# Output stores on GpSimd's queue and seven load buffers in the transformer stage of a Fourier tokenizer

## The chip, the cores and the metric

The kernel runs on one core of a Trainium2 chip. The metric is the device time of one execution in microseconds (us): the median of several runs. Three runs of the kernel before gave 12764.55, 12770.84 and 12775.92 us, so the time to compare with is 12770.84 us. One further execution was profiled; its trace spans 12772.9 us, and all times inside the trace are counted from its start.

## The reference

The input is 64 images of 256 x 256 and, for each, 77 text rows of 256. Everything is float32. Cut to what matters:

```
v = concat(x, gx, gy) @ p_w + p_b                      # 32 channels
for i in range(4):                                     # Fourier layers
    v = irfft2(low modes of rfft2(v) mixed over channels) + (v @ w_w[i] + w_b[i])
    v = batch_norm(v);  v = relu(v) if i < 3 else v
h = squeeze(v @ q_w + q_b)                             # one channel: 256 rows of 256
h = concat(h, txt)                                     # 333 rows (tokens) of 256
h = h + attention(layer_norm(h))                       # one head, width 256
z = layer_norm(h)
w = z @ wr + br;  the 165 tokens with the largest w are kept
h = h + z + scatter(w * mlp(z[kept]))                  # mlp: 256 -> 1024, gelu, -> 256
```

The batch norm's sums run over all images, so a Fourier layer must be done for all 64 images before the next can begin.

## The kernel before, in words

**The Fourier layers** (`forward_first`, `mix_weights`, `mix`, `layer`) take the first 9.8 ms. The change doesn't touch them. The last layer's image is never made in full: the transformer stage works from what layer 2 left in DRAM (`src`, 8 MB for each image) and from the mixed modes of layer 3 (`mix_d[L - 1]`, 48 x 1024 floats for each image).

**The transformer stage** is one loop over the 64 images. For one image:

- `image_rows` makes the one-channel image. L858 loads the mixed modes `am`. L860 multiplies them by `qrow` into the tile `amq`, and L864 sums over channels to `a1`. TensorE takes two small transforms (L866, L871) into the PSUM tile `hp`. Then for t = 0 to 7, L876 loads a tile `ch` of 1 MB (128 partitions x 8 KB) from `src`, and four matmuls of L878 add it to `hp`. The `ch` tiles come from the pool `inp`, which has five buffers, so five loads can be ahead of TensorE. When all eight tiles are in, ScalarE writes `h` (L883), and L884 loads the text rows into it.
- `attention` normalizes `h` (statistics L892/L893, square root on ScalarE L895, `az` L900), transposes it (L910, copied out of PSUM to `azT`, one half by ScalarE at L168 and the other by VectorE at L170), and goes on with L956 (scores' weights), L968 (scores), L975 (exp), L982 (values), L997 (transposed probabilities) and L1006. L1002 adds the bias `boB` to `h` on GpSimd, and L1009 adds the attention's result.
- `select` ranks the tokens: L922 to L927 put the weights of all tokens into a row on every partition, and nine VectorE instructions for each of three token groups (L936 to L947) count who is larger and write the one-hot tile `place`.
- `feed_forward` gathers the kept tokens (L1024, L1035), runs the two layers of the mlp (L1041, L1052), transposes back (L1062, copied to `ys`), scatters with L1071 and adds in L1074 to the tile `o`. Sixteen stores of 16 KB (L1079) and one of 77 KB (L1083) write `o` to the output.

**What sets the order.** The loop runs three images at once: in one turn it issues `image_rows(b + 2)`, `attention(b + 1)`, `feed_forward(b)` and `select(b + 1)`. The framework's planner merges these into one fixed order for each engine, from its own estimate of when each instruction's inputs are there; then it adds the semaphore waits. Each engine, and each queue of DMA issues, works strictly in that order. All loads and all stores of this stage are issued by SyncE (SP), whose queue is therefore shared: a store that waits for `o` holds back every load behind it. GpSimd has only L1002 and L1067 (`h1 += z`) in this stage, three instructions of each for an image.

Of the kernel before, what the change touches and what calls it, by code (L numbers as in the profile page):

```python
# [9 lines left out]
F32 = mybir.dt.float32  # L10
AF = mybir.ActivationFunctionType
ALU = mybir.AluOpType
# [4 lines left out]
S = 256  # L17
C = 32
M = 12
KX = 2 * M  # L20
L = 4
TXT = 77
TOK = S + TXT
HID = 1024
EPS = 1e-5
KEPT = max(1, int(0.5 * TOK)) - 1
# [103 lines left out]
def tile_fno_fusion_transformer(ctx: ExitStack, tc: tile.TileContext, a, cst_d, grid_d, out):  # L130
    nc = tc.nc
# [626 lines left out]
    src = vd[L % 2]  # L758
    s_, t_ = st
    tcon = ctx.enter_context(tc.tile_pool(name="tcon", bufs=1))  # L760
    inp = ctx.enter_context(tc.tile_pool(name="inp", bufs=5))
    tabt = tables(tcon, "exT", "tri", "cstt")
    EXT, MASK4, IOTA = tabt("exT"), tabt("mask4"), tabt("iota")
    TRI = tabt("tri").rearrange("p (t j) -> p t j", t=3)
    qrow = tcon.tile([128, C, 1], F32, name="qrow")
# [3 lines left out]
    junk = tcon.tile([128, C], F32, name="junkq")  # L769
# [78 lines left out]
    ap_ = ctx.enter_context(tc.tile_pool(name="ta", bufs=2))  # L848
    tp = ctx.enter_context(tc.tile_pool(name="tt", bufs=2))
# [3 lines left out]
    def psum():  # L853
        return pp.tile([128, 512], F32, name="pp")

    def image_rows(b):
        am = ap_.tile([2 * KX, 32 * C], F32, name="am")
        nc.sync.dma_start(am, mix_d[L - 1][b].rearrange("p k c -> (p k) c"))  # L858
        tmp = ap_.tile([2 * KX, C, 32], F32, name="amq")
        nc.vector.tensor_tensor(  # L860
            tmp, am.rearrange("p (o k) -> p o k", k=32), qrow[0:2 * KX].to_broadcast([2 * KX, C, 32]), ALU.mult
        )
        a1 = ap_.tile([2 * KX, 32], F32, name="a1")
        nc.vector.reduce_sum(a1, tmp.rearrange("p o k -> p k o"), axis=AX.X)  # L864
        ps = psum()
        nc.tensor.matmul(ps[0:32, 0:S], lhsT=a1, rhs=EXT[0:2 * KX], start=True, stop=True)  # L866
        y1 = ap_.tile([32, 2, 128], F32, name="y1")
        evict(y1.rearrange("k t p -> k (t p)"), ps[0:32, 0:S], 2)
        hp = pb_.tile([128, 2, S], F32, name="hp")
        for t in range(2):  # L870
            nc.tensor.matmul(  # L871
                hp[:, t, :], lhsT=y1[:, t, :], rhs=T4[0:32], start=t == 0, stop=False, skip_group_check=True
            )
        for t in range(8):
            ch = inp.tile([128, 4, 2, S], F32, name="ch")
            nc.sync.dma_start(ch.rearrange("p g r y -> p (g r) y"), src[b][:, t])  # L876
            for g in range(4):
                nc.tensor.matmul(  # L878
                    hp[32 * g:32 * g + 32], lhsT=win[:, 7 - t:39 - t], rhs=ch[:, g], start=False, stop=t == 7,
                    skip_group_check=True,  # L880
                )
        h = tp.tile([128, 3, D], F32, name="h")
        nc.scalar.activation(h[:, 0:2, :], hp, AF.Identity, bias=hbias, scale=1.0)  # L883
        nc.sync.dma_start(h[0:TXT, 2, :], a["txt"][b])  # L884
        return h
# [28 lines left out]
    def select(z):  # L914


        wcol = small.tile([128, 3], F32, name="wcol")
        ps = psum()
        for t in range(3):
            r = rows[t]  # L920
            junk = tp.tile([128, TOK], F32, name="junk")
            nc.vector.scalar_tensor_tensor(  # L922
                junk[:r, :D], z[:r, t, :], 1.0, wrB[:r], ALU.mult, ALU.mult, accum_out=wcol[:r, t:t + 1]
            )
            dg = tp.tile([128, 128], F32, name="dg")
            nc.vector.tensor_scalar(dg[:r, :r], ID[:r, :r], wcol[:r, t:t + 1], None, ALU.mult)
            nc.tensor.matmul(ps[:, toks[t]], lhsT=ONES[:r], rhs=dg[:r, :r], start=True, stop=True)  # L927
        wrow = tp.tile([128, TOK], F32, name="wrow")
        nc.vector.tensor_scalar(wrow, ps[:, :TOK], brB, None, ALU.add)
        fw = small.tile([128, 3], F32, name="fw")  # L930
        place = tp.tile([128, 3, KEPT], F32, name="place")
        for t in range(3):
            r = rows[t]
            junk = tp.tile([128, TOK], F32, name="junk")
            wc = small.tile([128, 1], F32, name="wc")
            nc.vector.scalar_tensor_tensor(  # L936
                junk[:r, :r], wrow[:r, toks[t]], 1.0, ID[:r, :r], ALU.mult, ALU.mult, accum_out=wc[:r]
            )
            gt = small.tile([128, 1], F32, name="gt")
            nc.vector.tensor_scalar(junk[:r], wrow[:r], wc[:r], None, ALU.is_gt, ALU.add, accum_out=gt[:r])  # L940
            eq = small.tile([128, 1], F32, name="eq")
            nc.vector.scalar_tensor_tensor(
                junk[:r], wrow[:r], wc[:r], TRI[:r, t, :], ALU.is_equal, ALU.mult, accum_out=eq[:r]
            )
            nc.vector.tensor_add(gt[:r], gt[:r], eq[:r])
            nc.vector.tensor_scalar(fw[:r, t:t + 1], gt[:r], float(KEPT), wc[:r], ALU.is_lt, ALU.mult)
            nc.vector.tensor_scalar(place[:r, t, :], IOTA[:r], gt[:r], None, ALU.is_equal)  # L947
        return fw, place
# [68 lines left out]
    def feed_forward(b, h1, z, fw, place):  # L1017

        zs = tp.tile([128, 2, KEPT], F32, name="zs")
        for dh in range(2):  # L1020
            ps = psum()
            for t in range(3):
                r = rows[t]
                nc.tensor.matmul(  # L1024
                    ps[:, :KEPT], lhsT=z[:r, t, 128 * dh:128 * dh + 128], rhs=place[:r, t, :],
                    start=t == 0, stop=t == 2,
                )
            evict(zs[:, dh, :], ps[:, :KEPT], 2)
        back = tp.tile([128, 2, TOK], F32, name="back")
        for c, k in enumerate(kept):  # L1030
            n = k.stop - k.start
            ps = psum()
            for t in range(3):
                r = rows[t]
                nc.tensor.transpose(ps[:n, toks[t]], place[:r, t, k], ID[:r, :r])  # L1035
            evict(back[:n, c, :], ps[:n, :TOK], 2)
        g = tp.tile([128, HID // 128, KEPT], F32, name="g")
        for hb in range(HID // 128):
            ps = psum()
            for dh in range(2):  # L1040
                nc.tensor.matmul(  # L1041
                    ps[:, :KEPT], lhsT=w1[:, dh, 128 * hb:128 * hb + 128], rhs=zs[:, dh, :],
                    start=dh == 0, stop=dh == 1,
                )
            nc.scalar.activation(
                g[:, hb, :], ps[:, :KEPT], AF.Gelu_apprx_tanh, bias=b1c[:, hb:hb + 1], scale=1.0
            )
        yT = tp.tile([128, 2, KEPT], F32, name="yT")
        for dh in range(2):
            ps = psum()  # L1050
            for hb in range(HID // 128):
                nc.tensor.matmul(  # L1052
                    ps[:, :KEPT], lhsT=w2[:, hb, 128 * dh:128 * dh + 128], rhs=g[:, hb, :],
                    start=hb == 0, stop=hb == HID // 128 - 1,
                )
            nc.scalar.activation(yT[:, dh, :], ps[:, :KEPT], AF.Identity, bias=b2c[:, dh:dh + 1], scale=1.0)
        ys = tp.tile([128, 2, D], F32, name="ys")
        for c, k in enumerate(kept):
            n = k.stop - k.start
            ps = psum()  # L1060
            for dh in range(2):
                nc.tensor.transpose(ps[:n, 128 * dh:128 * dh + 128], yT[:, dh, k], ID)  # L1062
            evict(ys[:n, c, :], ps[:n, :D], 2)
        o = tp.tile([128, 3, D], F32, name="o")
        for t in range(3):
            r = rows[t]
            nc.gpsimd.tensor_add(h1[:r, t, :], h1[:r, t, :], z[:r, t, :])  # L1067
            ps = psum()
            for c, k in enumerate(kept):
                n = k.stop - k.start  # L1070
                nc.tensor.matmul(  # L1071
                    ps[:r, :D], lhsT=back[:n, c, toks[t]], rhs=ys[:n, c, :], start=c == 0, stop=c == 1
                )
            nc.vector.scalar_tensor_tensor(  # L1074
                o[:r, t, :], ps[:r, :D], fw[:r, t:t + 1], h1[:r, t, :], ALU.mult, ALU.add
            )
        for g in range(4):
            for n in range(4):
                nc.sync.dma_start(  # L1079
                    out[b, 64 * n + 16 * g:64 * n + 16 * g + 16].rearrange("(p t) d -> p t d", t=2),  # L1080
                    o[32 * g + 8 * n:32 * g + 8 * n + 8, 0:2, :],
                )
        nc.sync.dma_start(out[b, S:TOK], o[0:TXT, 2, :])  # L1083

    hs = {n: image_rows(n) for n in range(min(2, B))}
    done = attention(hs.pop(0))
# [43 lines left out]
```

## Time and profile before

| Stretch or engine | measured |
| --- | --- |
| whole span | 12772.9 us |
| Fourier layers and their weights | to about 9880 us |
| transformer stage, first L1071 to last L1071 | 9969.9 to 12762.0 us |
| TensorE busy, of 2800 us from 9900 on | 2620.5 us |
| VectorE busy, same stretch | 1664.7 us |
| ScalarE busy, same stretch | 962.5 us |
| GpSimd busy, same stretch | 319.8 us |
| DMA engines, mean share in 10000 to 12500 us | 0.53 to 0.56 |

In these views PE is TensorE's matmuls and PEld its weight loads, DVE is VectorE, ACT is ScalarE, POOL is GpSimd, SPq is SyncE's queue. A timeline row gives start, length, engine, source line, operation, tiles written and read, the number of instructions merged into it, and in brackets the idle time of the engine before it with what ended that. A row of the waits gives the waiting engine and line, what it waited for, the total, how often, and the longest. In a table of stretches the columns after the engines' busy times are the clock granted to TensorE, the busy share of the DMA engines and their GB/s. A float32 matmul shows as two instructions, a transpose as one.

### The profile page before, as it was taken

How to read it: one execution, taken by the hardware profiler on the slowest of the kernel's cores; microseconds unless marked ns; L12 is line 12 of the kernel's file. 1: busy time of each engine (PE TensorE's matmuls, PEld its weight loads, DVE VectorE, ACT ScalarE, POOL GpSimd, SP SyncE). 2: the span in 40 equal slices, each digit the busy share in tenths (PEclk: the TensorE clock that was granted, in tenths of full speed). 3: DMA queues.
4: the chain of work that ended last, by engine and by line, in shares of the span. 5: the costliest groups of instructions: out<-in, count | busy, mean ns of one | idle time of the engine just before them, and what ended most of it. 6: DMA issues, size and time to landing. Idle time of an engine off the chain costs nothing. (4 is left out here: it accounts for less than half of the span.)

```text
span 12772.9 us, 405290 instructions
## 1 busy us (share of the span) xinstructions
PE 11352.8 (89%) x182038; PEld 5910.2 (46%) x182038; DVE 8759.3 (69%) x10531; ACT 6084.0 (48%) x10221; POOL 1010.8 (8%) x952
## 2 busy tenths in 40 slices
PE   4999999997799999999969999999995999999999
PEld 2444444443344444444434444444443666666666
DVE  4777777776777767677767777677775655555555
ACT  4555555555455555555545555455553333333333
POOL 1000000001100000000010000000001111111111
PEclk7999999998899999999979999999997999999999
DMA  6555555556899989888888988889988655555554
GB/s 189 201 204 205 198 198 204 199 203 204 326 354 350 352 342 348 341 344 345 345 284 345 356 343 347 341 347 353 351 348 279 218 192 202 206 203 198 191 198 158
DMA packets 574645, 3484.98 MB, mean 273 GB/s; under 512 B 79848, under 2 KB 133352, under 8 KB 175976
## 3 DMA queue, kind: packets, MB, share of 16 engines
q1 hardware_dynamic: 562304, 3427.04, 70.8%
q0 software_dynamic: 2304, 28.30, 1.0%
q8 instruction: 1424, 23.33, 0.7%
q10 hardware_dynamic: 8296, 3.72, 0.1%
q14 instruction: 317, 2.60, 0.1%
HBM read 1761.83 MB, written 1696.92 MB: 271 GB/s over the span
## 5 line engine op out<-in xcount | busy, mean ns | idle before, releaser
L656 ACT ACTIVATE ring<-ring 128x1024 f32<-128x1024 f32 x3072 | 3108.8, 1012 | 1184.6 <-PE ring L649 1147.8
L637 DVE STREAM_TRANSPOSE t<-vo 128x2048 f32<-128x2048 f32 x1536 | 3549.9, 2311 | 173.8 <-ACT vo L632 12.2
L649 PE MATMUL ring<-vo,w 32*32 32x512 f32 x49152 | 2840.7, 622 | 385.6 <-DVE zt L676 136.7
L632 ACT ACTIVATE vo<-ring 128x1024 f32<-128x1024 f32 x1536 | 1568.1, 1021 | 3052.2 <-PE ring L625 2393.8
L633 DVE TENSOR_SCALAR vo<-ring 128x1024 f32<-128x1024 f32 x1536 | 1858.4, 1210 | 615.8 <-PE ring L625 427.2
L666 PE MATMUL ring<-t,cst 32*32 32x512 f32 x49152 | 1872.9, 604 | 305.5 <-issue 303.7
L676 DVE STREAM_TRANSPOSE zt<-ring 128x1024 f32<-128x1024 f32 x384 | 712.1, 1925 | 1657.1 <-PE ring L666 1657.1
L649 PEld LDWEIGHTS ring<-vo,w 32*32 32x32 f32 x49152 | 763.7, 105 | 1892.5 <-issue 477.4
L666 PEld LDWEIGHTS ring<-t,cst 32*32 32x32 f32 x49152 | 974.9, 103 | 1162.8 <-issue 706.8
L625 PE MATMUL ring<-vin,ws 32*32 32x512 f32 x32768 | 1241.9, 608 | 22.2 <-issue 19.7
L584 POOL TENSOR_TENSOR ams<-am,sk 48x512 f32<-48x512 f32 x384 | 486.8, 1268 | 8541.3 <-DMA am<-mix 8199.5
L689 PEld LDWEIGHTS ring<-cst,zt 128*128 128x128 f32 x4608 | 534.7, 193 | 177.2 <-ACT vo L632 161.2
L656 ACT ACTIVATION_READ_ACCUMULATOR ring<-ring 128x1 f32 x3072 | 584.1, 190 | 0.0
L689 PE MATMUL ring<-cst,zt 128*128 128x96 f32 x4608 | 566.9, 280 | 8.8 <-DVE zt L676 8.8
L878 PE MATMUL hp<-ch,win 128*32 128x512 f32 x4096 | 537.2, 619 | 4.9 <-DMA ch<-v 4.9
L595 PE MATMUL ring<-ams,cst 49*128 49x512 f32 (+1 forms) x1536 | 391.6, 620 | 99.2 <-POOL ams L584 88.8
L625 PEld LDWEIGHTS ring<-vin,ws 32*32 32x32 f32 x32768 | 253.5, 103 | 408.3 <-issue 378.8
L892 DVE BATCH_NORM_STATS2 abs<-h 128x6 f32<-128x256 f32 (+1 forms) x192 | 75.8, 402 | 439.1 <-ACT h L883 439.1
L1041 PEld LDWEIGHTS pp<-zs,w 128*128 128x128 f32 x2048 | 291.3, 190 | 99.2 <-issue 68.8
L1041 PE MATMUL pp<-zs,w 128*128 128x165 f32 x2048 | 332.2, 310 | 0.0
L1052 PEld LDWEIGHTS pp<-g,w 128*128 128x128 f32 x2048 | 292.5, 189 | 73.6 <-issue 68.8
L412 PE MATMUL mps<-wm,xh 32*64 32x128 f32 (+1 forms) x4608 | 110.2, 356 | 239.6 <-DMA xh<-xh 109.0
(930 smaller groups left out, 11717.9 us busy)
## 6 DMA issues: line engine op xcount, KB each, us to landing
v<-vo SPq DMA_DIRECT2D x1536, 1024.0 KB
vin<-v SPq DMA_DIRECT2D x1024, 1024.0 KB
ch<-v SPq DMA_DIRECT2D x512, 1024.0 KB
mix<-ob SPq DMA_DIRECT2D x192, 256.0 KB
am<-mix SPq DMA_DIRECT2D x384, 96.0 KB
xin<-in_x_dram SPq DMA_DIRECT2D x16, 1024.0 KB
mv<-in_x_dram SPq DMA_DIRECT2D x256, 64.0 KB
out_dram<-o SPq DMA_DIRECT2D x1024, 16.0 KB
```

Source lines behind the costliest of these rows:

```text
L584: nc.gpsimd.tensor_tensor(ams[b % 2][hv], a_[hv], sk[hv].rearrange("p c k -> p (c k)"), ALU.mult)
L625: nc.tensor.matmul(ps[n][32 * j:32 * j + 32], lhsT=ws[32 * n:32 * n + 32], rhs=v[32 * n:32 * n + 32, 2 * j:2 * j + 2, :], start=False, sto ...
L632: nc.scalar.activation(of[:, 0:2], t2[0], AF.Relu)
L633: nc.vector.tensor_scalar(of[:, 2:4], t2[1], 0.0, None, ALU.max)
L637: nc.vector.transpose(t32[b, t // 2][:, :, 8 * (t % 2):8 * (t % 2) + 8, :].rearrange("p y s c -> p s y c"), o.rearrange("p s (y l) -> p s ...
L649: nc.tensor.matmul(ps[n][32 * j:32 * j + 32], lhsT=w4[i + 1][32 * n:32 * n + 32], rhs=o[32 * n:32 * n + 32, 2 * j:2 * j + 2, :], start=Tru ...
L656: nc.scalar.activation(t2[n], t2[n], AF.Square, accum_out=acc[:, at:at + 1])
L666: nc.tensor.matmul(ps[n][32 * j:32 * j + 32], lhsT=FYT[32 * n:32 * n + 32, k, :], rhs=t32[b, j][32 * n:32 * n + 32, k].rearrange("p s c -> ...
L676: nc.vector.transpose(zt[:, h].rearrange("p k c -> p c k"), t2[h].rearrange("p n (s c) -> p c (n s)", c=C),)
L689: nc.tensor.matmul(ps[:, 0, 96 * g:96 * g + 96], lhsT=zt[:, h, k0:k0 + 4, :].rearrange("p k c -> p (k c)"), rhs=FX[:, h, 48 * r:48 * r + 9 ...
L878: nc.tensor.matmul(hp[32 * g:32 * g + 32], lhsT=win[:, 7 - t:39 - t], rhs=ch[:, g], start=False, stop=t == 7, skip_group_check=True,)
L1041: nc.tensor.matmul(ps[:, :KEPT], lhsT=w1[:, dh, 128 * hb:128 * hb + 128], rhs=zs[:, dh, :], start=dh == 0, stop=dh == 1,)
```

## The change

It has three parts, all in the transformer stage.

1. The 17 output stores of each image are issued by GpSimd and no longer by SyncE, so that loads needn't stand behind stores that wait for `o`.
2. The pool `inp` has seven buffers and no longer five: seven of an image's eight `ch` tiles can be loaded ahead.
3. To make room for these, L860 writes its product into `am` itself (the tile `amq` is gone), and the tiles `junk` (three uses in `select`) and `g` (the mlp's hidden layer) have one buffer and no longer two.

```diff
-    inp = ctx.enter_context(tc.tile_pool(name="inp", bufs=5))
+    inp = ctx.enter_context(tc.tile_pool(name="inp", bufs=7))
...
-        tmp = ap_.tile([2 * KX, C, 32], F32, name="amq")
+        tmp = am.rearrange("p (o k) -> p o k", k=32)
         nc.vector.tensor_tensor(
-            tmp, am.rearrange("p (o k) -> p o k", k=32), qrow[0:2 * KX].to_broadcast([2 * KX, C, 32]), ALU.mult
+            tmp, tmp, qrow[0:2 * KX].to_broadcast([2 * KX, C, 32]), ALU.mult
         )
...
-            junk = tp.tile([128, TOK], F32, name="junk")
+            junk = tp.tile([128, TOK], F32, name="junk", bufs=1)
...
-        g = tp.tile([128, HID // 128, KEPT], F32, name="g")
+        g = tp.tile([128, HID // 128, KEPT], F32, name="g", bufs=1)
...
-                nc.sync.dma_start(
+                nc.gpsimd.dma_start(
                     out[b, 64 * n + 16 * g:64 * n + 16 * g + 16].rearrange("(p t) d -> p t d", t=2),
                     o[32 * g + 8 * n:32 * g + 8 * n + 8, 0:2, :],
                 )
-        nc.sync.dma_start(out[b, S:TOK], o[0:TXT, 2, :])
+        nc.gpsimd.dma_start(out[b, S:TOK], o[0:TXT, 2, :])
```

The planner works from the changed program, so the fixed order of every engine in this stage changes as well. The built program after shows that order, without any times.

More of the change, by code (lines that the diff above doesn't have):

```diff
@@ L933, in select @@
             r = rows[t]
-            junk = tp.tile([128, TOK], F32, name="junk")
+            junk = tp.tile([128, TOK], F32, name="junk", bufs=1)
             wc = small.tile([128, 1], F32, name="wc")
```

## The prediction

> **What bounds the kernel now.** I read the waits of TensorE in the steady part of the transformer stage first, from 10000 to 12700 us:
>
> ```profile
> PE pp L910 <- DVE az L900: 78.8, 54, 2.7
> PE pp L1071 <- DVE ys L170: 45.0, 59, 1.6
> PE pp L956 <- ACT azT L168: 19.2, 39, 0.7
> PE pp L1062 <- ACT yT L1056: 17.0, 60, 1.0
> ```
>
> No load is among them: TensorE, busy 93.6% here, hardly ever waits for `ch` itself. It waits for `az`, the normalized next image. Next, its timeline at that place in two images, a smooth early one and a typical later one:
>
> ```profile
> 10096.15 0.67 PE L910 MATMUL pp<-cst,az 128*128 128x128 f32 x5
> 10096.75 1.13 PE L871 MATMUL hp<-cst,y 32*128 32x256 f32 x4
> 10097.81 4.50 PE L878 MATMUL hp<-ch,win 128*32 128x512 f32 x40
> 10102.24 0.29 PE L910 MATMUL pp<-cst,az 77*128 77x77 f32 x1
> 10102.36 2.45 PE L956 MATMUL pp<-azT,wqk 128*128 128x333 f32 x8
> 10104.94 3.63 PE L968 MATMUL pp<-azT,qT 128*128 128x333 f32 x12
> ...
> 11073.00 1.92 PE L878 MATMUL hp<-ch,win 128*32 128x512 f32 x16
> 11077.22 0.83 PE L910 MATMUL pp<-cst,az 128*128 128x128 f32 x4 [2.30 <-DVE az L900]
> 11079.02 0.35 PE L910 MATMUL pp<-cst,az 77*128 77x77 f32 x2 [0.98 <-DVE az L900]
> 11079.89 4.81 PE L956 MATMUL pp<-azT,wqk 128*128 128x333 f32 x8 [0.52 <-ACT azT L168]
> 11084.50 4.31 PE L968 MATMUL pp<-azT,qT 128*128 128x333 f32 x12
> ```
>
> The later image loses 3.80 us in three gaps, and then L956 and L968 are slow. The table of stretches says why: the granted clock falls to one half.
>
> ```profile
> 11075.80:11079.20 3.40, 1.01 (x6) 0.58 (x6) 3.23 (x13) 0.00 (x0) 1.67 (x3) 1.00 0.65 185
> 11079.20:11086.00 6.80, 6.28 (x13) 3.89 (x13) 0.51 (x1) 1.51 (x3) 0.57 (x1) 0.50 1.01 426
> ```
>
> Why is `az` late? VectorE waits for `h`, and SyncE's queue, a little earlier, shows where `h` got stuck:
>
> ```profile
> 11065.20 0.43 DVE L892 BATCH_NORM_STATS2 abs<-h 128x6 f32<-128x256 f32 x1 [8.55 <-ACT h L883]
> ```
>
> ```profile
> 11028.12 5.64 SPq L1079 DMA_DIRECT2D out_dram<-o  x16
> 11033.86 0.30 SPq L1083 DMA_DIRECT2D out_dram<-o  x1
> 11034.25 2.56 SPq L876 DMA_DIRECT2D ch<-v  x5
> ```
>
> The loads stand behind 17 stores, which themselves stood waiting for `o`. So the planner has spread L878 in small groups through the whole turn, `h` of the next image is finished only near the turn's end, and statistics, square root and `az` come too late for L910.
>
> The price of a turn: I took the first L1071 of each image from TensorE's timeline. The 64 start at 9969.91 and end at 12762.03 us. The last two intervals (31.3 and 23.1 us) have no image to load; the other 61 are 2792.1 - 54.4 = 2737.7 us, a mean of 44.88. The first six are 40.3 to 41.5 (10092.08 to 10132.36 is 40.28), later ones alternate between 41 to 42 and 48 to 49.
>
> **What the Trainium skill says.** (1) "TensorE: Matmul & The Clock Gate", What's actually happening: the clock is gated to half after an idle window of about 3.4 us, on a free-running clock. The trace agrees on half and on multiples of 3.4 us (6.80 above), but not on a wholly idle window: laying the clock record over the gaps between matmuls, from 10050 to 12730 us every fall follows a 3.41 us window holding at least 1.43 us idle, and none follows 1.42 or less (windows taken to end 0.6 us before the switch). The measurement decides: 1.43 us. (2) "DMA: Bandwidth & Descriptors", Anatomy of one DMA — SWDGE (gpsimd) path: about 2.0 us fixed for a DMA from GpSimd plus bytes/436e3. GpSimd's weight loads landed in 6.0 us at the least, larger and four together. (3) Same page, Issuing engines are not separate DMA queues: another issuer saves only the time on the sequencer. Nothing in this trace contradicts that. (4) "SBUF — State Buffer", SBUF: two separate sides: VectorE and GpSimd lock a shared port pair against each other for a whole instruction. The trace agrees: the 128x128 L926 takes 742 ns on average, beside L1067 on GpSimd, where the 77x77 one at 11070.91 takes 250.
>
> **The change, part by part.** What matters is the new order. The built program has, for TensorE in every steady turn (matmul counts):
>
> ```
> L927 x2 | L866 | L927 | L910 x5 | L871 x2 | L878 x28 | L910 | L956 x2 (first half of azT) | L878 x4 | L956 x2 (second half) | L968 x6 | L982 x6 | L997 x9 | L1006 x9 | L1024 x6 | L1035 x6 | L1041 x16 | L1052 x16 | L1062 x4 | L1071 x6
> ```
>
> So seven `ch` tiles are used in one block, the eighth right after, and `h` is ready some 28 us earlier; VectorE's order has the next image's statistics and `az` between the maxima of L973, a turn ahead of L910. That removes the `az` gaps and with them the clock falls. It is the smooth early image over again. Now each step, with P the start of L927:
>
> *TensorE* (spacings of 10092 to 10132): L910 at P+1.37, L871 at P+1.97, L878 at P+3.03. A group of four takes 4.43/5 = 0.886, so seven take 6.20: P+9.23; L910 0.13; first half of L956 1.24, to P+10.6; the eighth group 0.9, to P+11.5. Then it needs the second half of `azT`.
>
> *VectorE* copies that half behind its whole `select` and behind L864 and L860. At 10012.93 (an early image with L864 there): the row of weights starts at P+1.57, L864 is done at P+3.87, `select` takes 16.80 to 21.74 = 4.94. After, its order is one token group after another, and each dependent pair costs about 0.11 more (L942 to L945 there 0.59 for 0.49), some six times: 5.5. L860 in between adds 1.13, the copy 0.5: P+11.0. Against P+11.5: no gap. But L1002 now comes after the stores and meets L860; at the price of L926, 0.5 each, I bound this at 0 to 0.8 us and take 0.4, just hidden. In-place L860 costs the same as before.
>
> *The eighth load.* SyncE's order has `am` (L858) ahead of it, which waits for L864 (P+3.9); it also waits for the first L878 group (P+3.9). Issued at P+4.4. DMA runs at 426 GB/s when full (row above), 1.05 MB in 2.5 us; the issue at 11034.25 showed data about 1 us later. Landed at P+8.4 to 10.2 (with stores between), needed at P+10.6. Seven more loads, 18 us, land long before the next block.
>
> *GpSimd.* An issue there:
>
> ```profile
> L361 POOL DMA_DIRECT2D wn<-in_L_tok_fw_dram x48: 489/489/674, 3095.8 to 9731.4; - x48
> ```
>
> 17 x 0.49 = 8.3 us from P on; each also waits for the landing of the store eight before it, which at 3 us is hidden by 8 x 0.49 = 3.9. L1002 (3 x 0.76) is done by P+10.6; L1009 needs it after L1006's first three matmuls, at about P+21. Ten us of slack. Other end: landings of 12 us would bring L1002 to P+27.
>
> *ScalarE*: L883 (0.69) now sits ahead of the copies `qT`, so L968 waits about 0.27 in place of 0.13. *Single `junk` and `g`*: VectorE is in order anyway (the 0.11s above); `g` is read by L1052 a turn earlier. *L1071*: its wait for `ys` is 0.4 where no L864 stands ahead, 1.0 to 1.6 where one does; after, none does: 0.4 always, as in the 40.28. *Fewer breaks of L878*: two groups fewer apart, 0.1 each, less.
>
> Sum for a turn: 40.28 + 0.14 - 0.2 + 0.3 for what `azT` or the eighth load leave = 40.5. End: the last 17 stores take 8.3 instead of 5.7 on the queue, and land: 11 us after L1071's end. Span: 9970 + 61 x 40.5 + 54.4 + 2.9 + 11 = 12509; 2 us less for the median over the span: 12507. I say 12510, 2.0% below 12770.84.
>
> **The rivals.** *B, a gap remains at L956*: if VectorE is 0.8 us or more later still, or the load is late, a gap of 1 to 2 us stays in each turn, and where it passes 1.43 us the clock falls in part of the turns (1.7 to 3.4 us each). A turn of 41.5 to 44, say 42.5: 12629. For it: VectorE's margin is half a us. Against: the eighth L878 group stands exactly there. *C, slower*: GpSimd's issues lock the shared port against VectorE's two-input instructions in `select`, or their landings delay L1002 and L1009. With 3 us more on VectorE, a 2.5 us gap and a fall of 6.8 us (3.4 lost) a turn is 40.5 + 2.5 + 3.4 = 46.4: 12867. For it: the port is shared; the trace shows no such issue beside `select`. Against: 10 us of slack, and issue times steady at 489 ns. *D, no change*, 12771: loads are hidden anyway (no wait for `ch` above 10 us in sum). Against: the wait was never for `ch` but for what the late `ch` made late.
>
> **How the numbers follow.** Forecast 0.73, B 0.13, C 0.11, D 0.03. Predicted 12510. Low: a turn of 40.0, 12480. High: a turn of 43, in the middle of B, 12660; beyond it lie C, D and half of B, some 0.2. Faster is the forecast and nearly all of B less what a slower B loses, 0.85; within 0.2%, 0.03; slower, 0.12.
>
> **What would show it.** Right: the wait of L910 for `az` near 0, granted clock 0.99 or more from 10000 us on, L1071 every 40 to 41 us, 28 L878 matmuls in one block without a wait, L1002 ending 8 us or more before L1009. Wrong: a gap before the second half of L956, or at the eighth L878 group on a DMA; L936, L942 or L860 longer than before; GpSimd's issues longer than 0.5 us or waiting on one another. What would make the prediction wrong is VectorE's path to `azT`, which has only half a us to spare.

## The result, and the profile after

The changed kernel takes 12472.96 us (median of 4 runs, 12446.06 to 12482.64), the kernel before beside it 12767.69 us: a ratio of 0.977, 95% interval 0.975 to 0.979. That is 295 us faster, and 37 us less than the 12510 predicted, just under the low end of 12480.

TensorE's waits after, from 10000 to 12700 us as before (waiting engine and line, what it waited for, total, times, longest):

```profile
PE pp L1071 <- DVE ys L170: 24.7, 61, 0.4
PE pp L1062 <- ACT yT L1056: 17.0, 63, 0.3
PE hp L878 <- DMA ch<-v: 4.5, 10, 1.1
PE pp L1024 <- DVE place L947: 3.0, 1, 3.0
```

The wait of L910 for `az`, 78.8 us before, is not there at all. That of L1071 for `ys` is down to 0.4 us each time. What is new in the list is 4.5 us for a load, in ten turns, and 3.0 us for `place`, once.

One turn of TensorE after:

```profile
11007.60 0.67 PE L910 MATMUL pp<-cst,az 128*128 128x128 f32 x5
11008.21 1.13 PE L871 MATMUL hp<-cst,y 32*128 32x256 f32 x4
11009.26 6.22 PE L878 MATMUL hp<-ch,win 128*32 128x512 f32 x56
11015.41 0.29 PE L910 MATMUL pp<-cst,az 77*128 77x77 f32 x1
11015.53 1.33 PE L956 MATMUL pp<-azT,wqk 128*128 128x333 f32 x4
11016.79 1.07 PE L878 MATMUL hp<-ch,win 128*32 128x512 f32 x8
11017.79 1.39 PE L956 MATMUL pp<-azT,wqk 128*128 128x333 f32 x4
11019.25 3.63 PE L968 MATMUL pp<-azT,qT 128*128 128x333 f32 x12
```

No row has an idle time in brackets. Seven `ch` tiles are used in one block, and the eighth between the halves of L956. The copy of `azT` that the second half needs ends at 11017.28, 0.5 us before it:

```profile
11016.79 0.49 DVE L170 COPY azT<-pp 128x333 f32<-128x333 f32 x1
```

The clock, in the table of stretches for 11500 to 12000 us, first the kernel before, then after (the third number from the right is the granted clock):

```profile
11500.00:12000.00 500.00, 465.00 (x2576) 306.10 (x2575) 287.43 (x1037) 165.22 (x331) 55.99 (x66) 0.93 0.53 193
```

```profile
11500.00:12000.00 500.00, 487.77 (x2972) 342.05 (x2971) 339.08 (x1221) 194.10 (x397) 163.41 (x282) 1.00 0.58 229
```

TensorE is busy 97.6% of the time in place of 93.0%, and at full speed: the clock record after has no fall between 9926 and 12441 us.

The turns, from the first L1071 of each image: 64 starts, from 9959.8 to 12460.55. The first 61 intervals have a mean of 40.09 us, where the kernel before had 44.88; most are 39.98 to 40.0. They account for 61 x 4.79 = 292 us, all of the gain. TensorE's idle time between 9960 and 12440 us fell from 153.8 us (55 turns, 2.8 each) to 62.1 (62 turns, 1.0 each): 1.8 us a turn, 110 in all. The time at half clock after 9960 us fell from 235 to 23 us (what is left lies in the last turns), worth half of the difference, 106 us. By subtraction some 76 us are left, which would be matmul time. L878 stands in 6 pieces in the median turn before and in 2 after; at 0.24 to 0.3 us for a piece (below) four pieces fewer in 61 turns make 59 to 73 us, an estimate.

### The profile page after: what moved, and what is told of

It reads as the page before. It is cut to its first block, busy times and chain, and to the rows that moved or that the text cites. A ratio compares the mean times of both kernels' runs of the same rounds, so it can differ in the third digit from the quotient of the medians.

```text
span 12476.6 us, 405217 instructions
## 1 busy us (share of the span) xinstructions
PE 11172.7 (90%) x182038; PEld 5874.2 (47%) x182038; DVE 8784.2 (70%) x10531; ACT 6065.1 (49%) x10217; POOL 1529.5 (12%) x2040
## 5 line engine op out<-in xcount | busy, mean ns | idle before, releaser
L1079 POOL DMA_DIRECT2D out_dram<-o x1024 | 512.3, 509 | 660.1 <-DVE o L1074 628.8
L878 PE MATMUL hp<-ch,win 128*32 128x512 f32 x4096 | 473.3, 602 | 8.6 <-DMA ch<-v 8.5
L883 ACT ACTIVATE h<-hp,hbias 128x512 f32<-128x512 f32 x64 | 44.0, 687 | 597.5 <-PE hp L878 581.4
L595 PEld LDWEIGHTS ring<-ams,cst 49*128 49x128 f32 (+1 forms) x1536 | 147.5, 188 | 349.8 <-issue 242.1
L1041 PE MATMUL pp<-zs,w 128*128 128x165 f32 x2048 | 302.4, 305 | 0.0
```

The lines of the kernel that those rows point to most:

```text
L595: nc.tensor.matmul(ps[:, n, :], lhsT=EX[hv, 128 * h:128 * h + 128], rhs=ams[b % 2][hv], start=True, stop=True, skip_group_check=True,)
L878: nc.tensor.matmul(hp[32 * g:32 * g + 32], lhsT=win[:, 7 - t:39 - t], rhs=ch[:, g], start=False, stop=t == 7, skip_group_check=True,)
L1041: nc.tensor.matmul(ps[:, :KEPT], lhsT=w1[:, dh, 128 * hb:128 * hb + 128], rhs=zs[:, dh, :], start=dh == 0, stop=dh == 1,)
```

## The experiments

My theory 1: the stores on SyncE's queue made the planner put L878 late, and taking them off is the gain. Rivals: theory 2, the seven buffers are the gain; theory 3, it is GpSimd as the issuer, or SyncE's time for issues. The first four kernels take the change apart. "Turn" below is the median of the first 61 intervals, and the column of L878 gives the matmuls of each piece in which a turn has it. Each ratio is to runs of the kernel before on the same chip (12762.35 us for all rows but the last, 12761.32 there).

| kernel | `ch` buffers | stores on | L878 | turn, us | time, us | ratio to before (95%) |
| --- | --- | --- | --- | --- | --- | --- |
| before | 5 | SyncE | spread | 45.38 | 12762 | 1 |
| room only | 5 | SyncE | spread | 44.31 | 12758.55 | 1.000 (0.999 to 1.001) |
| seven buffers | 7 | SyncE | spread | 44.30 | 12730.96 | 0.998 (0.997 to 0.999) |
| stores only | 5 | GpSimd | 20+4+4+4 | 40.56 | 12519.36 | 0.981 (0.980 to 0.983) |
| changed, but stores on ScalarE | 7 | ScalarE | 28+4 | 41.21 | 12598.88 | 0.987 (0.986 to 0.989) |
| changed, second time | 7 | GpSimd | 28+4 | 39.98 | 12467.15 | 0.977 (0.976 to 0.979) |

**Stores only**: the kernel before, with one edit.

```diff
-                nc.sync.dma_start(
+                nc.gpsimd.dma_start(
...
-        nc.sync.dma_start(out[b, S:TOK], o[0:TXT, 2, :])
+        nc.gpsimd.dma_start(out[b, S:TOK], o[0:TXT, 2, :])
```

> Only the seventeen stores go to GpSimd's queue; five load buffers, the separate scaled copy of the modes and the two buffers of junk and g stay as before. Theory 1 (the stores on SyncE's queue held the loads, and with them the order of L878, back): in this kernel's order of TensorE the groups of L878 stand together again, 20 + 4 + 4 + 4, and h is no longer late, so the waits of L910 for az go, the clock stays up through the transformer, the turn is 40.3 to 40.8 us and the time 12,480 to 12,530 us, 0.977 to 0.982 of before. Theory 2 (the seven load buffers bring the gain): about as before, 12,740 to 12,800 us, with waits of L910 left.

Measured 12519.36 us, a turn of 40.56, as theory 1 had it. TensorE's waits, 10000 to 12700 us:

```profile
PE pp L1071 <- DVE ys L170: 24.6, 61, 0.4
PE pp L1062 <- ACT yT L1056: 17.0, 63, 0.3
PE hp L878 <- DMA ch<-v: 10.5, 27, 1.4
```

L910 is gone from the list with five buffers still in place. The clock does not fall between 9930 and 12479 us. This part alone is 243 of about 295 us. The one edit changes two things together, the queue of the stores and, through the planner, the order of every engine.

**Seven buffers only**, the stores left on SyncE (the changed kernel, with the edit above undone):

> Seven load buffers, modes scaled in place and single junk and g, while the stores stay on SyncE's queue. Theory 1: the stores still hold the loads back, the order keeps L878 spread over the turn, L910 waits for az 75 to 80 us in all, the clock falls some 30 times; 12,730 to 12,800 us, within 0.3% of before. Theory 2 (the buffers bring the gain): 12,470 to 12,520 us.

Measured 12730.96 us, 31 us less than before. Theory 2 falls. The longest of TensorE's waits, 10000 to 12700 us:

```profile
PE pp L910 <- DVE az L900: 65.1, 63, 2.8
```

And SyncE's queue, in its waits from 9980 to 12400 us and in one turn:

```profile
SPq L1079 <- DVE amv L893: 858.5, 36, 33.7
SPq L876 <- PE hp L878: 390.3, 70, 12.6
SPq L1079 <- DVE o L1074: 296.5, 13, 28.1
SPq L1079 <- DVE ars L896: 123.8, 6, 20.7
```

```profile
11499.78 10.98 SPq L876 DMA_DIRECT2D ch<-v  x2
11532.96 6.05 SPq L1079 DMA_DIRECT2D out_dram<-o  x16
11539.12 0.30 SPq L1083 DMA_DIRECT2D out_dram<-o  x1
11539.51 3.09 SPq L876 DMA_DIRECT2D ch<-v  x6
```

The rows of L1079 add to 1279 of 2420 us: more than half of the time, the queue stands with a store at its head that waits for VectorE. (The row names the VectorE instruction that ended next to the release; at 11532.96 it is the second L1074, which ended at 11532.94, with an L893 begun at 11532.86.) In this turn six loads stand behind the stores. Seven buffers can't help while the loads that would fill them aren't issued. TensorE shows next to no wait for `ch` in these lists, because its own fixed order has L878 just as late.

This order isn't there from the start. In the first two turns of this kernel L878 stands as 28 + 4 matmuls, as in the changed kernel, and these turns take 40.48 and 39.89 us (the changed kernel: 39.98), although the stores are on SyncE's queue. Then the first block shrinks by four matmuls every turn or few, to 8 from the eleventh turn on, while the turn rises to 44.3. In the kernel before the same happens from 20 matmuls down to 8 or 12, and with the stores on GpSimd's queue it doesn't: there nearly every turn has the block of the table. So the time goes with the order, and not with the stores' standing on SyncE's queue as such: with the stores there, the planner lets L878 fall apart turn by turn, and seven buffers only put that off.

**Room only**: five buffers, stores on SyncE, but the modes scaled in place and `junk` and `g` single.

> The modes are scaled in place and junk and g have one buffer, with five load buffers and the stores on SyncE's queue: only what made room for the buffers. Theory 1 and theory 2 both say the time of before within 0.3% (12,730 to 12,800 us); should single junk and g cost waits on VectorE that reach TensorE, it is slower by up to 1 us in each of 61 turns, 12,830 us.

Measured 12758.55 us: nothing, as both theories had it, with the stores on SyncE's queue (with them on GpSimd's it is another matter, see the five buffers below).

**Stores on ScalarE's queue**:

```diff
-                nc.gpsimd.dma_start(
+                nc.scalar.dma_start(
...
-        nc.gpsimd.dma_start(out[b, S:TOK], o[0:TXT, 2, :])
+        nc.scalar.dma_start(out[b, S:TOK], o[0:TXT, 2, :])
```

> The changed kernel with the stores issued on ScalarE's queue in place of GpSimd's. Theory 1 (leaving SyncE's queue is what counts, not where to): the order keeps L878 together, so the clock stays up; ScalarE pays for the issues, 17 in each turn by 0.05 to 0.5 us of its time, which lies on the way of z and L910 where it comes late: 12,470 to 12,560 us. Theory 3 (GpSimd is what brings it, because [...]its stores don't share SyncE's way): 12,700 us and more.

Measured 12598.88 us: 163 us better than before, so GpSimd isn't needed for the larger part of the gain, and theory 3 falls in that form. But it is 39 us more than the 12,560 I allowed. The chosen issuer costs what it delays. ScalarE in a bad turn (the view begins after the first five of its sixteen stores), then TensorE in the same:

```profile
11028.02 10.26 ACTq L1079 DMA_DIRECT2D out_dram<-o  x11
11038.37 0.61 ACTq L1083 DMA_DIRECT2D out_dram<-o  x1
11039.09 0.69 ACT L883 ACTIVATE h<-hp,hbias 128x512 f32<-128x512 f32 x1 [15.41 <-DMA out_dram<-o]
11039.67 0.43 ACT L168 COPY azT<-pp 128x333 f32<-128x333 f32 x1
```

```profile
11037.32 1.06 PE L878 MATMUL hp<-ch,win 128*32 128x512 f32 x8 [1.49 <-DMA ch<-v]
11040.16 4.08 PE L956 MATMUL pp<-azT,wqk 128*128 128x333 f32 x8 [1.77 <-ACT azT L168]
```

ScalarE computes nothing for 15.4 us, and its half of `azT` comes late. This wait adds up to 92.5 us in 59 turns (10000 to 12500 us), and 15 falls of the clock follow between 9960 and 12440 us. TensorE's idle time there is 153.3 us, as much as before, and yet the time is 163 us less: a sum of idle time says little without where the gaps fall.

**Six and five buffers**: the changed kernel with `bufs=6`, then `bufs=5`, for what the cuts of L878 cost.

> The changed kernel with six load buffers in place of seven; its order for TensorE has L878 as 24 + 4 + 4 matmuls, where the changed kernel has 28 + 4 and the kernel with the stores alone 20 + 4 + 4 + 4. Theory A (each further piece that L878 is cut into costs about 0.3 us, worked out from the most frequent turns of those two, 40.56 and 39.98, over two pieces): a turn of 40.3, 12,490 us. Theory B (a piece costs 0.1 as predicted, and the rest of the difference is something else that the stores-alone kernel does): a turn of 40.1, 12,479 us.

> The changed kernel with five load buffers; L878 as 20 + 4 + 4 + 4, the stores on GpSimd's queue, modes scaled in place, single junk and g. Theory A (a piece costs 0.3): a turn of 40.55 to 40.6, 12,508 us, the same as the stores alone. Theory B (a piece costs 0.1): a turn of 40.2, 12,486 us; then single buffers or the place scaling were worth the rest.

Measured 12506.87 us (ratio 0.980, 0.979 to 0.982) and 12569.87 us (0.985, 0.984 to 0.986): both outside of what I expected, because a gap opened that neither theory had. With six and with five buffers the planner put no group of L878 between the halves of L956. With five, VectorE's copy, then TensorE:

```profile
11722.16 0.49 DVE L170 COPY azT<-pp 128x333 f32<-128x333 f32 x1
```

```profile
11719.84 1.33 PE L956 MATMUL pp<-azT,wqk 128*128 128x333 f32 x4
11722.71 1.39 PE L956 MATMUL pp<-azT,wqk 128*128 128x333 f32 x4 [1.54 <-DVE azT L170]
11724.02 1.06 PE L878 MATMUL hp<-ch,win 128*32 128x512 f32 x8
```

What hides the copy is L878 ahead of the second half: 20 of its matmuls with five buffers, 24 with six, all 32 in the changed kernel, and the gap is 1.54, 0.70 and 0 us. So the group between the halves does in the changed kernel what the prediction said.

The stores-only kernel has five buffers too, and it has a group of L878 between the halves (20 + 4 ahead of the second) and no gap in all but two turns. The two differ in the edits that made room alone: the in-place modes and the single `junk` and `g` cost about 50 us here (12519.36 to 12569.87 us) through the order that the planner makes of them, and nothing where the stores are on SyncE's queue.

To get at the cuts all the same I took each turn's idle time off, for all kernels (medians of the turns):

| kernel | pieces that L878 is cut into | turn | idle | busy |
| --- | --- | --- | --- | --- |
| eight buffers (below) | 1 | 39.77 | 0.73 | 39.04 |
| reduction twice (below) | 1 | 40.36 | 1.04 | 39.30 |
| stores on ScalarE | 1 | 41.21 | 1.86 | 39.35 |
| changed | 2 | 39.98 | 0.47 | 39.52 |
| six buffers | 3 | 40.55 | 0.96 | 39.59 |
| five buffers | 4 | 41.70 | 1.81 | 39.88 |
| stores only | 4 | 40.56 | 0.55 | 39.99 |

(Stores on ScalarE: planned as two pieces, 28+4 with the short L910 between them.) The idle column leaves out the 0.4 us that the next L1071 waits for `ys`, the same in all seven; the busy column has it. A further piece costs 0.07 to 0.35 us, 0.24 on average from 39.23 (mean at one) to 39.94 (mean at four). That is nearer to theory A's 0.3 than to the 0.1 predicted. It is rough: the three kernels with one piece differ by 0.31 among themselves, so their orders differ in more than the cuts.

**The stores one turn late**, back on SyncE:

```diff
-        feed_forward(b, *now)
+        o = feed_forward(b, *now)
+        if b:
+            store(b - 1, last)
+        last = o
...
+    store(B - 1, last)
```

> The changed kernel with the stores back on SyncE's queue, all 17 of them, but one turn later: image b - 1 is stored in the turn of image b, so that no store has to wait for o in front of a load. Theory 1 (the harm was the wait for o at the head of the loads' queue): h is early, no wait of L910 for az, no fall of the clock; L878 is in 16 + 4 + 4 + 4 + 4, three pieces more than the changed kernel at 0.2 to 0.3 us, a turn of 40.6 to 41.0, 12,510 to 12,540 us. Theory 3 (what counts is SyncE's time for 17 issues, 5.9 us a turn, or that the stores share the loads' queue at all): the time of before, 12,730 us or more.

Measured 12843.4 us, 1.007 of before (1.005 to 1.008): a miss of 300 us, and slower than before. The wait of L910 for `az` did go, as theory 1 had it. The first thirteen turns take 39.3 to 42.1 us, with L878 in one or two pieces at first, so SyncE's time for 17 issues is not what costs (theory 3). But the first block shrinks here too, and from 10510 us on another wait has taken the place in each turn:

```profile
11703.03 0.45 PE L927 MATMUL pp<-dg,cst 77*128 77x77 f32 x2 [0.47 <-DVE dg L926]
11704.90 1.03 PE L866 MATMUL pp<-cstt,a 48*32 48x256 f32 x2 [1.42 <-DVE a L864]
```

```profile
11705.00:11716.00 11.00, 11.00 (x36) 4.95 (x35) 6.43 (x30) 0.98 (x2) 0.00 (x0) 0.55 0.31 112
```

and SyncE's queue, from the same turn:

```profile
11711.99 7.83 SPq L1082 DMA_DIRECT2D out_dram<-o  x16
11719.93 0.29 SPq L1086 DMA_DIRECT2D out_dram<-o  x1
11720.26 0.34 SPq L858 DMA_DIRECT2D am<-mix  x1
```

Now `am` stands behind the stores. The planner has put L860 and L864 after the copy of `ys` and almost at the turn's end, although `am` is there long before (its last issue is 28 us ahead of the next L860). L866 waits for `a`, and the clock is at half for 10.2 us of each of these turns: 47.8 us. So one part of theory 1 was too narrow. Even stores that have nothing to wait for do harm on the loads' queue, by moving what stands behind them in the planner's order. That the wait for `o` is the cause was not shown by itself; that the stores' place on that queue is, was. No run moves the stores and keeps the order of the engines.

**VectorE's margin**: L864 done twice, the second time for the same sums.

```diff
-        nc.vector.reduce_sum(a1, tmp.rearrange("p o k -> p k o"), axis=AX.X)
+        for _ in range(2):
+            nc.vector.reduce_sum(a1, tmp.rearrange("p o k -> p k o"), axis=AX.X)
```

> The changed kernel with the reduction L864 done twice, 1.86 us more on VectorE ahead of the copy azT (the second writes the same sums). The order has all 32 matmuls of L878 in one block. If VectorE's margin before the second half of L956 is the half microsecond that the prediction worked out, a gap of 1.2 to 1.5 us opens there in each turn: a turn of 41.1 to 41.4 and 12,540 to 12,560 us where the clock holds, and up to 12,650 us where the gap passes 1.43 us and the clock falls for 3.4 us. If the margin is 2 us and more (rival), the time is 12,460 to 12,475 us.

Measured 12503.0 us (0.980, 0.979 to 0.981), between the two expectations. The planner moved L860 (1.21 us) out of the way, so that only 0.7 of the added 1.9 us was ahead of the copy. That ended 11.72 us after L927's start in place of 11.04, and the wait for `azT` was 0.3 us in such a turn. A margin of about half a us agrees, but the run doesn't measure it sharply.

**Eight buffers**: the changed kernel with `bufs=8`, and `zs`, `back`, `yT`, `ys` and `o` with one buffer each for room.

```diff
-    inp = ctx.enter_context(tc.tile_pool(name="inp", bufs=7))
+    inp = ctx.enter_context(tc.tile_pool(name="inp", bufs=8))
...
-        zs = tp.tile([128, 2, KEPT], F32, name="zs")
+        zs = tp.tile([128, 2, KEPT], F32, name="zs", bufs=1)
```

> The changed kernel with eight load buffers, so that a whole image can be loaded ahead; to make room zs, back, yT, ys and o have one buffer each. Its order for TensorE has all 32 matmuls of L878 in one block. Theory A (each piece that L878 is cut into costs 0.2 us of TensorE's time: 39.3, 39.5, 39.6 and 39.9 to 40.0 us of busy time in a turn for 0, 1, 2 and 3 extra pieces): busy 39.3, and with the 0.5 idle of the changed kernel a turn of 39.8, 12,460 us; a wait of L1006 for probT of 0.4, as the kernel with the doubled reduction shows in the same order, would take that back: 40.2, 12,480 us. Theory C (the eighth group between the halves of L956 hides the copy azT, and without it a gap opens there): 40.3 to 41 us, 12,490 us and more.

> The changed kernel itself, beside the next one on the same chip: 12,440 to 12,490 us, 0.977 of before, turns of 40.0 us.

Measured 12442.6 us (0.975, 0.974 to 0.977) against 12467.15 for the changed kernel on the same chip; the runs, 12437 to 12456 and 12462 to 12480, don't overlap. It is the fastest kernel here, by 0.2%; the turn of 39.77 is theory A's. One turn of TensorE:

```profile
11713.22 7.07 PE L878 MATMUL hp<-ch,win 128*32 128x512 f32 x64
11720.22 0.28 PE L910 MATMUL pp<-cst,az 77*128 77x77 f32 x1
11720.34 2.45 PE L956 MATMUL pp<-azT,wqk 128*128 128x333 f32 x8
...
11730.35 4.25 PE L1006 MATMUL pp<-v,probT 128*128 128x256 f32 x18 [0.39 <-ACT probT L168]
```

L878 is in one piece, and L956 has no gap (theory C falls; the copy ended at 11721.25, 11.06 us after L927's start). From the start of L878 to that of L968 this turn takes 9.64 us, where the changed kernel takes 9.99; from L997 to L1024, with the wait of 0.39 for `probT`, 5.51 where that takes 5.37. So 0.35 is saved and 0.14 lost.

## Why the prediction was right in direction and 37 us off

**What held.** The cause, the order after and its consequences: no wait for `az`, no falling clock, L1071 every 40 to 41 us, 28 matmuls of L878 in one block. Taking the stores away from SyncE is the gain, shown by kernels with and without it: 243 us with five buffers, 264 with seven, and 189 with five and the edits that made room, where the gap at L956 opens. The steps with a time: the copy of `azT` ready at P+11.0 (measured 11.04), and the eighth load issued at P+4.4. The 17 stores took GpSimd to P+8.7, where 8.3 was said; landings did not hold them up except in a few turns. Rival B (a gap at L956) did not come about in the changed kernel but did with five buffers, 1.54 us in size. Rival C asked for a lock on VectorE. L942 (128x333) took 568 ns in the median beside the stores, 560 before and 567 with the stores on ScalarE's queue; L936 (128x128) 283 beside them and 283 with those on ScalarE's: no lock to be seen. Rival D falls with the time.

**What failed: the size of the turn.** I added 40.28 + 0.14 - 0.2 + 0.3 = 40.5; it is 40.09. Laid beside the smooth turn of 40.28, step by step:

| term | predicted | measured |
| --- | --- | --- |
| fewer cuts of L878: L878 7.42 to 7.15; L1006 -0.16, L1024 1.89 to 1.69, L1041 4.73 to 4.53; L956, cut now, +0.20 | -0.2 | -0.63 |
| what `azT` or the eighth load leave | +0.3 | 0 in most turns, 0.1 in the mean |
| L968's wait for `qT`: 0.13 to 0.07 | +0.14 | -0.06 |
| L1006's wait for VectorE's half of `probT` | not foreseen | +0.39 |

The first term is the step that was mis-sized. I counted "two groups fewer apart, 0.1 each"; the smooth turn has four pieces and the changed one two, and the two made 0.63, some 0.3 each. Here is one cut in the smooth turn:

```profile
10112.00 3.30 PE L1006 MATMUL pp<-v,probT 128*128 128x256 f32 x14
10115.23 1.07 PE L878 MATMUL hp<-ch,win 128*32 128x512 f32 x8
10116.23 1.09 PE L1006 MATMUL pp<-v,probT 128*77 128x256 f32 x4
10117.16 1.29 PE L1024 MATMUL pp<-place,fz 128*128 128x165 f32 x8
```

The 0.1 is L878's own side: a group that stands alone takes 1.00 us, where one in a block takes 0.886. The prediction put the other side at nothing: the matmuls that are interrupted lose too. L1006 takes 3.23 + 0.93 = 4.16 us here, and 4.00 where nothing stands in it (11044.80 to 11048.80 in the kernel before).

The second term, 0.3, was an allowance beside a working that itself showed no gap, and the working was right. The third had the wrong sign: L883 does stand ahead of the copies `qT`, and yet L968 waits for only 0.07 us in every turn. L956 and its wait together came out 0.14 us longer, just the size predicted, but through the cut of L956: that is luck. The fourth was left out. VectorE's order has the next image's statistics and `az` between the maxima, which the prediction says, but not what they delay. In the turn shown above VectorE works without a gap from 11021.80 us on, its half of `probT` comes late, and TensorE waits (in the smooth turn this copy starts at 10111.86, ahead of L1006):

```profile
11026.58 0.49 DVE L170 COPY probT<-pp 128x333 f32<-128x333 f32 x1
```

```profile
11026.31 4.55 PE L1006 MATMUL pp<-v,probT 128*128 128x256 f32 x18
11030.70 1.85 PE L1024 MATMUL pp<-place,fz 128*128 128x165 f32 x12
```

The copy ends at 11027.07, and L1006's second matmul starts at 11027.13 after an idle time of 0.12 us, too short for the lists of waits. So L1006 takes 4.39 us and not 4.00; 56 of 61 turns have such an idle time.

The terms add to -0.30, so a usual turn is 39.98, and the mean is 40.09. 61 turns at 0.41 less make 25 us. The rest: the first L1071 came 10 us earlier than before (9959.8 for 9969.9), but two profiles of the very same changed kernel have it at 9959.8 and 9945.1, so that is scatter, which my low end of "a turn of 40.0" had no room for. The last two intervals and the end took 3 us more. -25 - 10 + 3 = -32: 12509 becomes the profiled 12477. The other 5 us of the 37 are the median, which lies 4 us under the profiled span where I had 1 above it.

**A step that failed without harm.** I had L1002 done by P+10.6, right after the stores, with ten us of slack before L1009. GpSimd in a usual turn (P is 11046.22):

```profile
11046.41 8.04 POOL L1079 DMA_DIRECT2D out_dram<-o  x16 [9.84 <-DVE o L1074]
11054.44 0.54 POOL L1083 DMA_DIRECT2D out_dram<-o  x1
11062.96 2.18 POOL L1002 TENSOR_TENSOR h<-h,boB 128x256 f32<-128x256 f32 x3 [7.98 <-DVE az L900]
```

L1002 writes into `h`, so it has to wait until L900 has read it: P+16.6 to P+18.9. L1009 starts at P+22.1, so the slack is 3.2 us and not 10. I had looked at what stands ahead of L1002 on its engine, and not at who still reads what it overwrites.

## What to carry to other kernels

A store that shares a queue with prefetches changes more than the queue: where a planner fixes the order of all engines, it moves the consumers of the loads behind it, and here next to no wait for a load then showed in the profile. Look for stores at the head of a load queue, and give them to an engine with time to spare on which nothing urgent follows; the same stores on ScalarE lost nearly half of the gain. Then look at the new order once more, since each small edit moved some other instruction onto the path (the five-buffer kernel and the late stores both did), and price a cut on both of its sides.

## What had not been expected of the hardware

- **The clock.** The prediction read 1.43 us of idle time in a 3.41 us window as the bound for a fall. The figure comes out of the trace of before, but it didn't carry over. With five buffers 56 turns have a gap over 1.43 us (median 1.54), and the clock stayed at 1.00 from 9960 to 12530 us:

```profile
11717.00:11724.00 7.00, 5.46 (x37) 2.07 (x29) 6.00 (x27) 0.43 (x1) 3.98 (x8) 1.00 1.01 369
```

  With the late stores gaps of 0.47 and 1.42 us, close together, came with a fall of 10.2 us in each turn from 10510 us on; counted in the prediction's windows these falls follow only 1.01 to 1.13 us of idle time. The Trainium skill's "TensorE: Matmul & The Clock Gate", What's actually happening, asks for an idle window; no run here had one in these turns, and the clock fell all the same. What besides idle time counts stays open. The gap with no fall lies amid the dense L956, the others beside small matmuls (L866, L910, L927); that this matters is a guess and not shown.
- **The shared port.** In the changed kernel the 128x128 L926 takes 286 ns in the median of 63 cases with no instruction of GpSimd beside it, and 626 in the 64 cases with L1067 beside it; before, 126 of 128 had L1067 beside them and took 751. That agrees with what the page "SBUF — State Buffer", SBUF: two separate sides, says of two engines that lock each other out. Issues of stores on GpSimd had no such effect (above).
- **Stores from GpSimd.** An issue took 508 ns in the median, and a store of 16 KB landed in 3.0 us (1.7 to 7.4). "DMA: Bandwidth & Descriptors", Anatomy of one DMA — SWDGE (gpsimd) path, would give about 2.0 plus 0.04 us as an estimate; the measured 3.0 decides.
